# Four graph layers on one core: an order of issue from a planner, replaced by an order written as one mark per operation

## The chip, the cores and the metric

The kernel runs on one core of a Trainium2 chip. The metric is the device time of one execution in microseconds, given as the median of several runs. An execution that the hardware profiler took gives the profile and the trace. The engines are TensorE (PE, with its weight loads as PEld), VectorE (DVE), ScalarE (ACT), GpSimd (POOL) and SyncE (SP), which only issues DMA transfers here.

## The reference

The input `x` is 128 graphs of 64 nodes with 256 features in float32, and `adj` is a 64x64 matrix of zeros and ones for each graph. Four graph layers follow one another, and each is wrapped as `x = layernorm(x + layer(x))`:

```
layer 0: h = x; five times:
             m = h @ weight[l];  agg = A^T m
             r = sigmoid(i_r + h_r);  z = sigmoid(i_z + h_z)
             n = tanh(i_n + r * h_n);  h = (1 - z) * n + z * h
layer 1: agg = eps * x + adj @ x;  h = silu(rmsnorm(agg @ W1 + b1));  out = h @ W2 + b2
layer 2: t = artanh(|x|) * x / |x|;  s = adj @ t
         out = project(tanh(|s|) * s / |s|)
layer 3: h = x @ W^T + b;  u = adj * exp(e_i + f_j + a_b)
         out = (u / sum(u)) @ h
```

In layer 0 `i` and `h` stand for the two products with the recurrent cell's weights, `w_ih` and `w_hh`. Everything is float32.

## The kernel before

Two graphs of 64 nodes make a block of 128 rows, four blocks make a group of 512 rows, and 16 groups cover the input. Each group goes through all four layers on its own. Three sets of buffers (`NF = 3`) let up to three groups be under way together, so that one group's matmuls can lie beside another's vector work. [...]

The Python code does not issue instructions as it goes. Every step (`pe`, `turn`, `dve`, `act`, `pool`, `copied`, `scaled`, L319 to L350) adds an operation, an `Op`, to the list of its stream. Stream 0 prepares constants and weights, and the 16 groups follow as one stream each (L1167 to L1170). An `Op` knows the engines that can do it, an estimated duration, and through `either` (L174) which operations must come before it. Most have one engine. A copy out of PSUM (`copied`, L335 on ACT or L336 on DVE) and a scaling with a bias (`scaled`, L340 on ACT or L341 on DVE) have two, and so have `tan` (L1082, L1083) and `hw` (L1145, L1147).

`Flow.issue` (L225) then sets the order. A planner, `Plan.advance` (L70), keeps an estimated clock for each engine and chooses, again and again, the operation that can start first, among the first few of each engine (`AHEAD`) in four streams (`WINDOW`). Ties and priorities go by one of three ranks. The string `CHOICES` has one digit for each stretch of 5 us of the planner's clock and says which rank holds in it. The operations are issued in that order, and each instruction is tied behind the one before it on its engine (L238), so that the order on every engine, the queue of SP among them, is the planner's. Within this order an engine waits for what its next instruction needs, and everything behind that instruction waits with it.

These steps matter around the change:

- In layer 0 `gated` (L759) runs five times for each group. `gate` (L798) makes the matmuls of L802 into the banks `p_ga`, `p_gb` and `p_gc`; `prod` (L807) those of L808 into `p_hx`, `p_hy`, `p_ix` and `p_iy`. `taken` (L848) and `plus` (L851) bring them into `U` and `V`; `begun` (L819) and `added` (L823) into `hnb`. `sums` (L783) makes the differences `tA` and `tB` on DVE by the helper at L347.
- Between two of the five rounds DVE transposes `h` into `t` (L764), and four DMA transfers on SP (`moved`, L677) bring it into `hr`. `aggregate` (L680) multiplies that by the edges, into `ps_agg`.
- `load` (L375) issues a group's loads on SP: eight of `xs` (L382), four of `x` (L387) and four of `edge` (L391).
- A layer norm (`layer_norm`, L703) takes its statistics from ACT (L716, L719) or, in the last two groups, from DVE (L723 to L725), a power from POOL (L727), and scales the rows (L340 or L341).
- Layer 1 makes `hid` by the matmuls of L985, squares it (L971), scales it on DVE (L1034) and applies the activation on ACT (L1036). The matmuls into `ps_o1` follow (L1044, recorded at the helper's line L317, the name without its digits being `ps_o`).
- POOL adds a bias to whole rows and sums squares by the helper at L350.
- Layer 2 has a logarithm (L1063) and a tanh (L1101) on ACT, each with its own table of functions to be loaded where the table in place has not got it. `tan` (L1082) feeds `ps_sup`.
- Layer 3 takes transposed rows `x3T`, over DMA transfers or in the last two groups by TensorE (`ps_T`, L659), and goes through `ps_a`, `hw` (L1142, L1145) and `ps_att` to the stored rows (L1165).

Of the kernel before, what the change touches and what calls it, by code (L numbers as in the profile page):

```python
# [23 lines left out]
BANKS = 8  # L24


class Buf:


    def __init__(self, make, slot=None, bank=False):  # L30
        self.make, self.slot, self.bank = make, slot, bank
        self.ap, self.uses, self.left, self.after = None, [], 0, ()
# [8 lines left out]


class Op:
    __slots__ = ("eng", "us", "run", "ways", "stream", "n", "kb", "sets", "need", "then", "bufs", "opens", "id", "way", "port")

    def __init__(self, ways, stream, n, kb, sets, port=()):
        self.port = port
        self.ways = {eng: (us, run) for eng, us, run in ways}
        self.eng, self.us, self.run = ways[0]
        self.stream, self.n, self.kb, self.sets = stream, n, kb, sets  # L50
        self.need, self.then, self.bufs, self.opens, self.id, self.way = 0, [], (), None, 0, 0.0


class Plan:


    def __init__(self, flow):
        self.flow = flow
        ops = [o for s in flow.streams for o in s]
        self.need = [o.need for o in ops]  # L60
        self.at = [0.0] * len(ops)
        self.uses = {}
        self.clock = dict.fromkeys(flow.AHEAD, 2.5)
        self.queues = [{e: deque(o for o in s if e in o.ways) for e in self.clock} for s in flow.streams]
        self.banks = [0.0] * BANKS
        self.left, self.first, self.bus = len(ops), 0, 0.0
        self.lands = [0.0] * flow.TRANSFERS
        self.order, self.table, self.port = [], None, 0.0

    def advance(self, until, rank):  # L70


        flow, need, at, clock, banks = self.flow, self.need, self.at, self.clock, self.banks
        while self.left and clock["PE"] < until:
            best = None
            for s in range(self.first, min(self.first + flow.WINDOW, len(self.queues))):
                for e, q in self.queues[s].items():
                    opened = False
                    for _, o in zip(range(flow.AHEAD[e]), q):
                        t = max(clock[e], at[o.id], self.port) if e in o.port else max(clock[e], at[o.id])  # L80
                        if o.opens is not None:
                            if opened or not banks or need[o.id]:
                                opened = True
                                continue
                            t = max(t, banks[0])
                        elif need[o.id]:
                            continue
                        elif o.kb and e != "POOL":
                            t = max(t, self.lands[0])
                        elif o.sets and self.table not in o.sets:  # L90
                            t += flow.TABLE
                        key = (t + flow.SOONER if len(o.ways) > 1 and e == "DVE" else t, *rank(s, o))
                        if best is None or key < best[0]:
                            best = key, o, e, t
            if best is None:
                return False
            _, o, eng, t = best
            if o.sets and self.table not in o.sets:
                self.table = o.sets[0]
            for e in o.ways:  # L100
                self.queues[o.stream][e].remove(o)
            self.order.append((eng, o))
            end = t + o.ways[eng][0]
            clock[eng] = end
            if eng in o.port:
                self.port = end
            if o.opens is not None:
                banks.pop(0)
            for b in o.bufs:
                n = self.uses.get(b, b.left) - 1  # L110
                self.uses[b] = n
                if not n:
                    banks.append(end + flow.hop(eng, "PE"))
                    banks.sort()
            if o.kb:
                self.bus = max(self.bus, end + flow.DMA[0]) + o.kb / flow.DMA[1]
                end = self.bus + flow.DMA[2]
                if o.eng != "POOL":
                    self.lands = [*self.lands[1:], end]
            for u in o.then:  # L120
                need[u.id] -= 1
                at[u.id] = max(at[u.id], end + flow.hop(eng, u.eng))
            self.left -= 1
            while self.first < len(self.queues) and not any(self.queues[self.first].values()):
                self.first += 1
        return True


class Flow:

    AHEAD = {"PE": 32, "DVE": 10, "ACT": 10, "POOL": 4, "SP": 2}


    HOPS = {"from PE": 0.22, "to PE": 0.36, "else": 0.06, "own": 0.0}

    REACH = {"from PE": 0.22, "to PE": 0.15, "else": 0.06, "own": 0.0}

    SOONER = 0.4


    DMA = (2.0, 330.0, 1.0)
    TRANSFERS = 8

    TABLE = 1.28
    WINDOW, STRETCH, LAGS = 4, 5.0, (60.0,)
    CHOICES = ("0110000002200022000010000001110100000000000101100022010011000220121010001100020002021101200021110012"
               "2211210220202220001022000200012200202011010110010000000101100002211011022212100001101010000001011210"
               "0001000010110112002210001201201100100000011000021111000100100010102011000201200012220100000001221100"
               "0010010012010011000000010100000010011021010000010200100021000011011210000100101202022101121200000011"
               "11100101011110111111010001011111100111111111100100010000")  # L160

    BEHIND = mybir.DependencyInfo(mybir.DependencyClass.NoSync, mybir.DependencyReason.DATA)

# [7 lines left out]
    def op(self, eng, us, run, w=(), r=(), kb=0, sets=None, port=False):  # L171
        self.either([(eng, us, run)], w, r, kb, sets, (eng,) if port else ())

    def either(self, ways, w, r, kb=0, sets=None, port=()):  # L174

        o = Op(ways, len(self.streams) - 1, len(self.ops), kb, sets, port)
        before = set()
        for accesses, writes in ((r, False), (w, True)):
# [26 lines left out]
            u.then.append(o)  # L205
        self.ops.append(o)

    def hop(self, e, to, hops=None):
        hops = hops or self.HOPS
        if e == to:  # L210
            return 0.0 if e == "PE" else hops["own"]
        return hops["from PE" if e == "PE" else "to PE" if to == "PE" else "else"]

    def ways(self):

        for i, o in enumerate(o for s in self.streams for o in s):
            o.id = i
        path = {}
        for ops in self.streams:
            longest = 0.0  # L220
            for o in reversed(ops):
                path[o] = o.us + max((path[u] + self.hop(o.eng, u.eng, self.REACH) for u in o.then if u.stream == o.stream), default=0.0)
                o.way = longest = max(longest, path[o])

    def issue(self):  # L225
        self.ways()
        ranks = (lambda s, o: (s, o.n), lambda s, o: (s if o.kb else -s, o.n), *(lambda s, o, lag=lag: (lag * s - o.way, s, o.n) for lag in self.LAGS))
        plan, until = Plan(self), 0.0
        for c in self.CHOICES:
            until += self.STRETCH  # L230
            assert plan.advance(until, ranks[int(c)])
        assert not plan.left
        last = {}
        for eng, o in plan.order:
            made = o.ways[eng][1]()
            for i in made if isinstance(made, list) else [made]:
                if eng in last:
                    self.tc.add_manual_dep(i.ins, last[eng].ins.name, self.BEHIND, reason="the plan's order")  # L238
                last[eng] = i
# [963 lines left out]
```

## Time and profile before

| what | value |
|---|---|
| median of three runs | 2290.74 us (2290.71 to 2294.59) |
| the profiled execution | 2295.18 us, of which the span from first to last instruction is 2293.4 us |
| mean granted TensorE clock | 0.992 |
| busy: PE, DVE, ACT, POOL | 2248.4, 1770.4, 1306.2, 338.3 us |
| matmul instructions | 11242 |
| DMA | 84.20 MB, mean 37 GB/s |

A row of the profile gives a source line, the engine, the operation, what it writes and reads, how often, and how long. After it stands in brackets how long the engine was idle just before, and which instruction's end released it. A row of the order of time begins with the start and the length in microseconds. Matmuls overlap one another, and their ends are modelled: the busy time of PE covers gaps that are shorter than one matmul's length. The starts of consecutive matmuls show those gaps. A line can be that of a helper (L317, L347, L350, L802, L808), so that the names of the tiles tell the rows apart.

### The profile page before, as it was taken

Reading aid. Unit: us, or ns where it says so; the run is one execution under the profiler, and the core shown is the slowest. Engines: PE = TensorE matmul, PEld = TensorE weight load, DVE = VectorE, ACT = ScalarE, POOL = GpSimd, SP = SyncE. Lnnn points to the kernel's source line nnn. Section 1 sums busy time; section 2 is a strip of 40 time slices with the busy share of each in tenths; the row PEclk is TensorE's granted clock in tenths of the full one; section 3 lists DMA queues with packets and bytes.
Section 4 is the critical chain, followed back from the end, with each engine's and each line's share of the span. In section 5 each row is a group of like instructions: output and inputs, shape, how many; then the busy total and the mean of one; then the engine's idle time right before and its main releaser. Section 6 shows DMA issues by size and latency. Waiting matters only on the chain.

```text
span 2293.4 us, 32317 instructions
## 1 busy us (share of the span) xinstructions
PE 2248.4 (98%) x11242; PEld 1978.7 (86%) x11242; DVE 1770.4 (77%) x4167; ACT 1306.2 (57%) x2797; POOL 338.3 (15%) x272
## 2 busy tenths in 40 slices
PE   9999999999999999999999999999999999999985
PEld 6888888888888888888888888888888888888874
DVE  6777788788778777778777878777787877877875
ACT  3444556675565655565655656555565665654665
POOL 3100202310110211112110111211102120110111
PEclk9999999999999999999999999999999999999997
DMA  5221112122112122121211212112131211212110
GB/s 146 33 28 29 28 19 58 19 49 38 40 28 57 21 28 49 19 53 28 31 43 28 49 29 49 28 21 47 28 58 19 36 41 29 49 19 28 22 26 19
DMA packets 428770, 84.20 MB, mean 37 GB/s; under 512 B 399124, under 2 KB 427824, under 8 KB 428608
## 3 DMA queue, kind: packets, MB, share of 16 engines
q1 hardware_dynamic: 426880, 80.26, 19.9%
q8 instruction: 89, 1.46, 0.3%
q10 hardware_dynamic: 1328, 1.31, 0.2%
q0 software_dynamic: 400, 0.57, 0.1%
q14 instruction: 73, 0.60, 0.1%
HBM read 32.55 MB, written 8.39 MB: 18 GB/s over the span
## 4 chain that ended last, share of the span: by engine, by line
PE 93%; DVE 4%; DMA 1%; ACT 1%; issue 0%; SPq 0%; POOL 0%; POOLq 0%; ACTq 0%; DVEq 0%
PE p_ga L802 24%; PE p_gc L802 12%; PE ps_o L317 9%; PE ps_agg L317 7%; PE p_ix L808 6%; PE p_gb L802 6%; PE p_hx L808 6%; PE p_ah L985 4%; PE p_iy L808 4%; PE p_hy L808 4%; PE ps_a L317 2%; PE p_ch L985 2%; PE ps_sup L317 1%; PE ps_wmih L317 1%; PE p_bh L985 1%; PE ps_att L317 1%
## 5 line engine op out<-in xcount | busy, mean ns | idle before, releaser
L727 POOL TENSOR_TENSOR rstd<-ve,pow 128x4 f32<-128x4 f32 (+1 forms) x64 | 76.6, 1197 | 1241.7 <-DVE ve L719 1192.1
L317 PE MATMUL ps_o<-w2s,hid 128*128 128x256 f32 x1024 | 232.4, 382 | 7.0 <-ACT hid L1036 7.0
L317 PEld LDWEIGHTS ps_o<-w2s,hid 128*128 128x128 f32 x1024 | 195.3, 191 | 34.4 <-ACT hid L1036 7.8
L340 ACT ACTIVATE hnb<-p_hx,half_b 128x256 f32<-128x256 f32 x214 | 100.6, 470 | 136.8 <-PE p_hx L808 103.2
L802 PE MATMUL p_gc<-tB,w_a 128*128 128x256 f32 x640 | 172.9, 379 | 1.0 <-DVE tB L347 1.0
L802 PE MATMUL p_ga<-tA,w_h 128*128 128x256 f32 x640 | 172.2, 380 | 0.0
L802 PE MATMUL p_gc<-tA,w_h 128*128 128x256 f32 x640 | 170.2, 379 | 0.0
L802 PE MATMUL p_ga<-tB,w_a 128*128 128x256 f32 x640 | 169.4, 380 | 0.8 <-DVE tB L347 0.8
L802 PE MATMUL p_ga<-hT,w_h 128*128 128x256 f32 x640 | 169.0, 379 | 0.7 <-DVE U L852 0.7
L802 PE MATMUL p_ga<-agg,w_a 128*128 128x256 f32 x640 | 167.5, 379 | 0.0
L317 PEld LDWEIGHTS ps_agg<-edge,hr 128*128 128x128 f32 x1024 | 140.5, 192 | 10.8 <-issue 1.3
L317 PE MATMUL ps_agg<-edge,hr 128*128 128x128 f32 x1024 | 142.9, 276 | 0.3
L855 ACT ACTIVATE U<-U,half_b 128x512 f32<-128x512 f32 (+1 forms) x160 | 94.3, 628 | 83.3 <-DVE U L852 83.2
L802 PEld LDWEIGHTS p_ga<-tB,w_a 128*128 128x128 f32 x640 | 120.7, 190 | 17.7 <-DVE tB L347 1.6
L802 PEld LDWEIGHTS p_gc<-tB,w_a 128*128 128x128 f32 x640 | 120.5, 190 | 17.3 <-DVE tB L347 1.4
L802 PEld LDWEIGHTS p_gc<-tA,w_h 128*128 128x128 f32 x640 | 120.2, 190 | 15.6
L802 PEld LDWEIGHTS p_ga<-agg,w_a 128*128 128x128 f32 x640 | 120.0, 190 | 15.6 <-ACT agg L335 0.2
L802 PEld LDWEIGHTS p_ga<-hT,w_h 128*128 128x128 f32 x640 | 119.0, 190 | 16.0 <-DVE U L852 1.1
L802 PEld LDWEIGHTS p_ga<-tA,w_h 128*128 128x128 f32 x640 | 117.2, 190 | 13.6
L855 ACT ACTIVATE V<-V,half_b 128x256 f32<-128x256 f32 (+1 forms) x160 | 87.8, 586 | 64.5 <-DVE V L852 64.0
L335 ACT COPY agg<-ps_agg 128x512 f32<-128x512 f32 x134 | 77.5, 579 | 62.7 <-PE ps_agg L317 61.5
L868 DVE TENSOR_TENSOR V<-p_ix,V 128x256 f32<-128x256 f32 x192 | 80.5, 420 | 31.1 <-PE p_ix L808 27.8
(259 smaller groups left out, 5480.4 us busy)
## 6 DMA issues: line engine op xcount, KB each, us to landing
hr<-t SPq DMA_DIRECT2D x256, 128.0 KB, 3.8
x<-in_x_dram SPq DMA_DIRECT2D x64, 128.0 KB, 2.6
xr<-in_x_dram SPq DMA_DIRECT2D x16, 512.0 KB, 4.0
out_dram<-x_n SPq DMA_DIRECT2D x16, 512.0 KB, 2.9
xs<-in_x_dram SPq DMA_DIRECT2D x120, 64.0 KB, 2.4
x3T<-t SPq DMA_DIRECT2D x56, 128.0 KB, 3.8
edge<-in_adj_dram SPq DMA_DIRECT2D x64, 32.0 KB, 2.3
wm<-in_L_gnn_weight_dram SPq DMA_DIRECT2D x5, 256.0 KB, 5.1
```

The source lines that it names most:

```text
L317: return nc.tensor.matmul(o, lhsT, rhs, start=(k == 0), stop=(k == nk - 1))
L335: flow.either([("ACT", 0.22 + 0.00077 * n, lambda: nc.scalar.copy(o(), i())), ("DVE", 0.145 + 0.00105 * n, lambda: nc.vector.tensor_copy(o ...
L340: flow.either([("ACT", 0.3 + 0.0008 * n, lambda: nc.scalar.activation(o(), i(), AF.Identity, bias=bias(), scale=scale())), ("DVE", 0.145 + ...
L727: pool(1.25, lambda: nc.gpsimd.tensor_tensor(rstd[:, :m, :], ve[:, :m, :], pow2[:, :m, :NB], OP.pow), [rstd], [ve])
L802: pe(HR, lambda i=i, w=w, c=c: nc.tensor.matmul(ps[:, c * HR:(c + 1) * HR], w[:, m, c * P:(c + 1) * P], v[i][0](), start=first and i == 1 ...
L808: pe(HR, lambda: nc.tensor.matmul(ps[:, j * HR:(j + 1) * HR], w[:, m, :], v[0](), start=first, stop=True, skip_group_check=True), [ps], [( ...
L855: act(HR if len(w) == 1 else R, lambda: nc.scalar.activation(o(), src(), AF.Tanh, bias=half_b[:, i * KD + c:i * KD + c + 1], scale=0.5), w ...
L868: dve(HR + 44, lambda: nc.vector.tensor_add(uu[:, c, half(n)], region(ps, j), uu[:, c, half(n)]), [(uu, (n, c))], [ps, (uu, (n, c))])
L985: pe(HR, lambda c=c: nc.tensor.matmul(ps[:, c * HR:(c + 1) * HR], w1f[:, w, (2 * q + c) * P:(2 * q + c + 1) * P], v[0](), start=first and ...
```

## The change

The planner goes: the class `Plan`, the estimates for hops between engines, DMA transfers and table loads, the ranks, and the string `CHOICES`. In their place stands `ORDER`, a string of marks, one for each operation, in the order of issue. A mark is one of 80 signs, or `~` with two of them for a larger number. It gives an engine, a stream counted from the first one that is not done, and a place among that stream's operations that still wait for that engine. `placed` reads the marks and hands out the operations in turn. The operations themselves, what they need, and the tie behind the one before on the same engine stay as they are. The string has 12850 marks.

```diff
-class Plan:
...
-    def advance(self, until, rank):
...
 class Flow:
...
-    AHEAD = {"PE": 32, "DVE": 10, "ACT": 10, "POOL": 4, "SP": 2}
...
-    WINDOW, STRETCH, LAGS = 4, 5.0, (60.0,)
-    CHOICES = ("0110000002200022000010000001110100000000000101100022010011000220121010001100020002021101200021110012"
...
+    ENGINES, AHEAD = ("PE", "DVE", "ACT", "POOL", "SP"), 6
+    SIGNS = "ABCDEFGHIJKLMNOPQRSTUVWXYZabcdefghijklmnopqrstuvwxyz0123456789!#$%&()*+,-./:;<=>"
+    ORDER = ("EACEDEAACCh#AAhAiDAAAAAAAAE~Bt$Ci~Bt~BOAAE888~Bti~Btli88888iE~BL~EtE~BL~BL~Et~BL~Bt~D8~CU~BLE~CU~DA~"
...
+    def placed(self):
+
+        at, n = self.SIGNS.index, len(self.SIGNS)
+        waiting = [{e: [o for o in s if e in o.ways] for e in self.ENGINES} for s in self.streams]
+        first, marks = 0, iter(self.ORDER)
+        for c in marks:
+            i = at(next(marks)) * n + at(next(marks)) if c == "~" else at(c)
+            i, e = divmod(i, len(self.ENGINES))
+            i, s = divmod(i, self.AHEAD)
+            o, eng = waiting[first + s][self.ENGINES[e]][i], self.ENGINES[e]
+            assert not o.need
+            for u in o.then:
+                u.need -= 1
+            for e in o.ways:
+                waiting[o.stream][e].remove(o)
+            while first < len(waiting) and not any(waiting[first].values()):
+                first += 1
+            yield eng, o
+        assert first == len(waiting)
 
     def issue(self):
-        self.ways()
...
-        plan, until = Plan(self), 0.0
-        for c in self.CHOICES:
-            until += self.STRETCH
-            assert plan.advance(until, ranks[int(c)])
-        assert not plan.left
         last = {}
-        for eng, o in plan.order:
+        for eng, o in self.placed():
             made = o.ways[eng][1]()
```

## The prediction

> **What bounds the kernel now.** I read the page first (engines, slices), then the busy time by stage, then who TensorE waits for, and last the order of time where it waits.
>
> ```profile
> PE 2248.4 (98%) x11242; PEld 1978.7 (86%) x11242; DVE 1770.4 (77%) x4167; ACT 1306.2 (57%) x2797; POOL 338.3 (15%) x272
> PE   9999999999999999999999999999999999999985
> PEclk9999999999999999999999999999999999999997
> ```
>
> TensorE is the bound: 98% busy, and below nine tenths only in the last two of 40 slices. A new order of the same matmuls can win only what lies between them. The busy time by stage (columns: stretch, length, busy time of PE, PEld, DVE, ACT, POOL, granted clock, DMA share, GB/s) says where that is.
>
> ```profile
> 0.00:100.00 100.00, 95.85 (x463) 77.57 (x464) 63.80 (x153) 37.98 (x84) 26.59 (x48) 1.00 0.39 97
> 100.00:2150.00 2050.00, 2043.39 (x10307) 1811.80 (x10306) 1607.08 (x3722) 1185.64 (x2543) 291.50 (x209) 1.00 0.20 35
> 2150.00:2250.00 100.00, 87.68 (x404) 73.81 (x402) 73.55 (x187) 59.87 (x120) 13.02 (x10) 0.95 0.11 22
> 2250.00:2293.00 43.00, 21.44 (x72) 15.52 (x72) 26.00 (x107) 22.69 (x53) 7.18 (x6) 0.68 0.07 25
> ```
>
> Idle: 4.2 us in the first 100, 6.6 in the next 2050, 12.3 in the next 100, 21.6 in the last 43, where the clock also falls. Busy time hides small gaps because matmuls overlap, so I also took the starts of consecutive matmuls: a 128x256 one follows the last after 216 ns, and what exceeds such steady distances is lost. That gives a loss of 4.3 us up to 100; 14.6 from 100 to 2150, of which nine places of over 0.3 us make 7.6 and the rest is crumbs; 12.8 plus 4.4 at half clock from 2150 to 2243; 16.3 plus 5.9 at half clock from there to the last matmul start at 2283.1; and 10.3 after it. Steady matmuls need 2223 us and the first starts at 2.5; that adds up to the span but for rounding.
>
> ```profile
> PE ps_sup L317 <- ACT tan L1082: 8.9, 1, 8.9
> PE ps_o L317 <- ACT hid L1036: 7.0, 3, 4.3
> PE ps_T L659 <- ACT x_n L340: 4.9, 2, 3.5
> ```
>
> The three longest waits all lie after 2190. The 4.3 is an order on DVE, here at its place:
>
> ```profile
> 2192.78 0.74 DVE L944 SCALAR_TENSOR_TENSOR ea<-ident,eps_c,adjT 128x512 f32<-128x512 f32 x1
> ...
> 2194.64 0.39 DVE L723 BATCH_NORM_STATS2 st<-y 128x6 f32<-128x256 f32 x1
> ...
> 2196.41 2.06 DVE L1034 SCALAR_TENSOR_TENSOR hid<-hid,cols,ps_rms 128x512 f32<-128x512 f32 x3
> ```
>
> ```profile
> 2193.01 0.63 PE L669 MATMUL ps_hr<-ident,hT 128*128 128x128 f32 x4
> 2197.97 0.79 PE L317 MATMUL ps_o<-w2s,hid 128*128 128x256 f32 x1 [4.33 <-ACT hid L1036]
> ```
>
> DVE does one group's layer-norm statistics before another group's three `hid`, and TensorE's next matmul needs those `hid`.
>
> **The change part by part.** Decoding the marks by the rule in `placed` gives 5794 PE, 3725 DVE, 2457 ACT, 266 POOL and 608 SP operations. The trace of before has 266 POOL and 608 SP operations too, its 11242 matmul instructions are 5794 operations (two each, a transpose one), and its ACT instructions make 2465 operations. So nothing is added or removed, and net eight operations that either engine can do go from ACT to DVE. A copy costs 0.58 us on ACT (L335) and 0.68 on DVE (L336): 5.4 us more on DVE, hidden under its 23% idle. If that cover failed, 5.4 would be the whole price. I take 0.
>
> How far is the order moved? A POOL mark tells how many PE operations are placed before it, and the trace of before tells how many had started when the same-numbered POOL instruction ran. From the 43rd POOL operation on, the two mostly differ by two or less. The last eight, the powers of the two final groups' norms, stand 70, 48, 44, 40, 40, 21, 3 and 0 PE operations before the end, against some 70, 49, 44, 42, 40, 20, 10 and 0. So the interleave of the groups stays; single steps are shuffled inside it.
>
> *Start* (4.3 lost): weights must land first; I take 0.5 back, ends 0 and 2.
>
> *Middle.* What can return is the 7.6 us of nine places; the crumbs (7.0) are no order. Five of the nine, 4.4 us, follow a stretched DVE instruction:
>
> ```profile
> 1176.41 2.84 DVE L347 TENSOR_TENSOR tB<-agg 128x512 f32<-128x512 f32 x1
> 1179.29 0.42 DVE L347 TENSOR_TENSOR tB<-agg,tB 128x256 f32<-128x256 f32 x1
> ```
>
> ```profile
> 1176.36 2.35 POOL L350 TENSOR_TENSOR xb<-x_n,b_r 128x1024 f32<-128x1024 f32 x1 [4.11 <-ACT x_n L340]
> ```
>
> `tB` takes 2.84 us instead of some 0.68 because POOL began 0.05 us before it, and TensorE lost 1.2. In the whole trace 32 DVE instructions are over 0.3 us above their median, all beside a POOL one, 29.4 us in sum, 0.92 each. [...] by the rows TensorE paid 0.46 to 1.17 in each of the five, mean 0.88, since other groups' matmuls cover the rest. I use 0.88. Half of the 7.6 back is 3.8; ends +7.6 and minus some ten new collisions, -8.8.
>
> *Approach, 2150 to 2243* (17.1 lost). Were the three `hid` (2.06 us) put before the statistics, TensorE would start about 3.5 us earlier, and the other group's chain be 2 us later; L1036 and L985 give several such swaps. The clock counts with it. [...] The trace has it falling at 2162.7 with no gap longer than 1.2 us before it, only several in a row, so the measurement decides: small gaps cost clock too. [...] by the trace it is 17.1. I take half, 8.5; ends 0 and 15.
>
> *Tail, from 2243* (22.2 lost, 10.3 after). It is one group's chain with too little of the other's matmuls beside it.
>
> ```profile
> 2263.75 0.59 ACT L335 COPY x3T<-ps_T 128x512 f32<-128x512 f32 x1 [0.31 <-PE ps_T L659]
> 2264.35 1.28 ACT L1101 ACT_TABLE_LOAD   x1
> 2265.64 0.21 ACT L1101 ACTIVATE th<-n 128x4 f32<-128x4 f32 x1
> ```
>
> The last group's tanh has its input at 2262.3 and stands behind two copies of the other group: before them it would come 1.4 us earlier. Layer-norm rows shared out to DVE (L341, 0.41 us) instead of four on ACT (L340, 2.07 together) give another 1 to 2. I take 3, ends -2 and 7. The 10.3 (residual, norm, store) is a chain in itself: 0.
>
> *DMA queue.* The order on SP can be read from its marks alone, as each group's list is in the code: the four `edge` loads of at least five groups now stand ahead of a block of `hr` transfers that they followed. Behind them wait those `hr`, and behind these `ps_agg`. A block of `edge` issues holds SP 2.6 us, so 13 us at worst, nothing if the SP queue was idle. TensorE's waits name no `hr` now and 1.6 us of `x3T`; two other groups' matmuls lie beside each transfer. I take 0. For new waits anywhere I subtract 2.
>
> **Sum.** 0.5 + 3.8 + 8.5 + 3 - 2 = 13.8 us. The profiled execution took 2295.2 (its span 2293.4), 4.4 over the median 2290.7; from it I get 2281.4, and from the median 2276.9. Forecast 2277.
>
> **Rivals.**
> *Only the middle moves* (2289, chance 0.12). The last groups' phases keep their places, and if the swaps there were no better the end keeps its 39 us: 3.8 - 2, within 0.2%. Against it: the longest waits are so plainly local that single moves reach them.
> *The end closes up* (2261, 0.15): 15 of the approach, 7 of the tail, 7 of the middle, 1 of the start, 30 in all. For it: a fix early in the chain moves all behind it, and the clock stays up. Against it: the unchanged interleave, with too few matmuls left to fill the last 40 us.
> [...] where the shuffled DVE steps fall under POOL's additions (L350, 2.35 us for 128x1024, L350 on `sqt` as well), TensorE pays 0.88 each. If only the middle's gain of 3.8 is had, ten more than now make it slower by over 0.2%; fifteen give 2300. Against it: five reach TensorE today among 256 POOL instructions, which keep their places.
>
> **How the numbers follow.** The forecast's case has 0.65, by itself 2266 to 2286. Faster by over 0.2% (below 2286.2): 0.65 + 0.15 = 0.80; within, 0.12; slower, 0.08. About 0.2% is what measuring this kernel can tell from no change. For 8 in 10 the range leaves out about half of the closed end (0.07), the collisions (0.08) and the upper part of the second case (0.05): 2262 to 2289.
>
> **What would show it.** The wait of `ps_o` for `hid` (7.0) halved and the stretch 2150 to 2243 some 8 us shorter, clock above 0.95 there; the tanh load ahead of the copies; the long waits of the middle at 4 us or less; 32 stretched DVE instructions, give or take ten. It is wrong if the approach keeps 12 us of waits, if TensorE waits for `hr`, or if stretched DVE instructions double.

## The result and the profile after

The changed kernel takes 2282.21 us (median of five runs, 2281.37 to 2283.47), the one before 2290.74 beside it (five runs, 2289.69 to 2294.59). By these medians it is 8.5 us faster. The ratio, of the means, is 0.9961 with a 95% interval of [0.9946, 0.9975], which makes 8.9 us. The profiled execution took 2281.37 us, its span 2279.6. Most line numbers of steps are 66 higher than before.

The page's engines and slices, after:

```profile
PE 2244.8 (98%) x11242; PEld 1974.4 (87%) x11242; DVE 1773.6 (78%) x4175; ACT 1307.2 (57%) x2789; POOL 337.6 (15%) x272
PE   9999999999999999999999999999999999999996
PEclk9999999999999999999999999999999999999997
```

The count of matmuls is the same, eight instructions have gone from ACT to DVE as the marks said, and only the last slice is now below nine tenths. Busy time by stage, after, with the same columns as before:

```profile
0.00:100.00 100.00, 97.34 (x466) 78.96 (x467) 63.92 (x155) 38.14 (x84) 25.90 (x48) 1.00 0.39 97
100.00:2150.00 2050.00, 2045.95 (x10319) 1812.00 (x10318) 1614.10 (x3739) 1188.89 (x2539) 291.28 (x209) 1.00 0.20 35
2150.00:2250.00 100.00, 84.78 (x396) 70.83 (x394) 76.50 (x212) 64.95 (x135) 15.81 (x12) 0.94 0.11 22
2250.00:2280.00 30.00, 16.74 (x64) 12.63 (x64) 19.05 (x71) 15.18 (x34) 4.58 (x4) 0.73 0.10 35
```

A reader could take the third row for a failure: PE is less busy there (84.8 against 87.7) and the clock no higher (0.94 against 0.95). But the row is cut at fixed times, and everything now comes earlier, so that some of the poorly filled tail has moved into it. To compare the same work I used the start of the n-th matmul in both traces. Against before, the 5000th starts 2.1 us earlier, the 10500th (at 2097) 4.0, the 10960th (at 2201) 13.1, the 11120th 10.5 and the last 13.6. So most of what the two traces differ by comes between 2097 and 2201, some is given back behind it, and the tail returns that. Who TensorE waits for, after:

```profile
PE ps_sup L383 <- ACT tan L1148: 8.3, 1, 8.3
PE ps_o L383 <- ACT hid L1102: 4.5, 3, 1.6
...
PE ps_T L725 <- ACT x_n L406: 1.4, 1, 1.4
PE ps_T L725 <- DVE x_n L407: 1.3, 1, 1.3
...
PE ps_rms L1096 <- POOL fac L1093: 0.8, 1, 0.8
```

The 4.3 us wait for `hid` is gone; three of 1.4 to 1.6 are left. The wait for the rows of `x_n` fell from 4.9 to 2.7, now with one row on DVE. A wait for `fac` is new. The order of time on DVE and on TensorE at the place that the prediction showed, now some 8 us earlier:

```profile
2178.52 1.41 DVE L1100 SCALAR_TENSOR_TENSOR hid<-hid,cols,ps_rms 128x512 f32<-128x512 f32 x2
...
2182.50 0.74 DVE L1100 SCALAR_TENSOR_TENSOR hid<-hid,cols,ps_rms 128x512 f32<-128x512 f32 x1
...
2185.48 0.73 DVE L1100 SCALAR_TENSOR_TENSOR hid<-hid,cols,ps_rms 128x512 f32<-128x512 f32 x1
```

```profile
2184.82 1.13 PE L383 MATMUL ps_o<-w2s,hid 128*128 128x256 f32 x4 [1.44 <-ACT hid L1102]
...
2186.23 2.78 PE L383 MATMUL ps_o<-w2s,hid 128*128 128x256 f32 x12
2190.43 1.56 PE L383 MATMUL ps_o<-w2s,hid 128*128 128x256 f32 x6 [1.41 <-ACT hid L1102]
```

Before, one `hid` was scaled and then six steps on `hT`, the rows `y`, `ea` and the statistics followed ahead of the next three. Now two are scaled ahead of the `hT` steps, one among them, one among the statistics. So 12 matmuls stand where TensorE had waited 4.33 us, and a wait of 1.41 us is left behind them. In the tail, on ACT:

```profile
2251.12 1.28 ACT L1167 ACT_TABLE_LOAD   x1
2252.42 0.20 ACT L1167 ACTIVATE th<-n 128x4 f32<-128x4 f32 x1
2252.53 1.06 ACT L401 COPY x3T<-ps_T 128x512 f32<-128x512 f32 x2
```

The tanh and its table load now stand ahead of the two copies.

### The profile page after: what moved, and what is told of

The parts are those of the page before. It is cut to its first block, busy times and chain, and to the rows that moved or that the text cites. A ratio compares the mean times of both kernels' runs of the same rounds, so it can differ in the third digit from the quotient of the medians.

```text
span 2279.6 us, 32289 instructions
## 1 busy us (share of the span) xinstructions
PE 2244.8 (98%) x11242; PEld 1974.4 (87%) x11242; DVE 1773.6 (78%) x4175; ACT 1307.2 (57%) x2789; POOL 337.6 (15%) x272
## 4 chain that ended last, share of the span: by engine, by line
PE 94%; DVE 3%; ACT 1%; DMA 1%; SPq 1%; issue 0%; POOL 0%; POOLq 0%; ACTq 0%; DVEq 0%
PE p_ga L868 23%; PE p_gc L868 11%; PE ps_o L383 10%; PE ps_agg L383 7%; PE p_gb L868 6%; PE p_ix L874 6%; PE p_hx L874 6%; PE p_ah L1051 4%; PE p_iy L874 4%; PE p_hy L874 4%; PE ps_a L383 3%; PE p_ch L1051 2%; PE ps_sup L383 1%; PE ps_wmih L383 1%; PE p_bh L1051 1%; PE ps_att L383 1%
## 5 line engine op out<-in xcount | busy, mean ns | idle before, releaser
L868 PE MATMUL p_gc<-tA,w_h 128*128 128x256 f32 x640 | 175.4, 379 | 0.0
L868 PE MATMUL p_ga<-hT,w_h 128*128 128x256 f32 x640 | 174.3, 380 | 0.2
```

Of the source, the lines that this page charges most:

```text
L868: pe(HR, lambda i=i, w=w, c=c: nc.tensor.matmul(ps[:, c * HR:(c + 1) * HR], w[:, m, c * P:(c + 1) * P], v[i][0](), start=first and i == 1 ...
```

## The experiments

Both orders can be written as marks. There are many places in the two strings at which both have placed the same set of operations, and there one can be continued by the other. I cut behind marks 11967, 12308, 12545 and 12589. In the trace of before, TensorE comes to these cuts at about 2118, 2180, 2226 and 2236 us. "Old" and "new" below are the two strings of 12850 marks. My theory: the gain is in the last groups' phases, where two chains share DVE and ACT, and little of it before the first cut. The first rival: the collisions in the middle, where a DVE instruction is stretched beside a POOL one, give it. The second: it comes from the engines that were exchanged, or from the code that hands out the operations, not from the order. Ratios are to the kernel before on the same chip, with 95% intervals, and gains in microseconds are worked out from them.

**The old order, written as marks.**

```diff
-ORDER = new marks 1 to 12850
+ORDER = old marks 1 to 12850
```

> The order of before written out as marks, so that the instructions and their order are those of before. Every theory expects a ratio of 1.000 within 0.002. What it is for is a second trace of that order: the profiled execution of before took 2295.2 us, 4.4 over the median. If the 4.4 us sits in the approach and the tail (matmul 10700 of 11242 starts within 0.5 us of the 2137 us of before), the gain of the end is overstated by the first pair of traces; if it sits in the middle (matmul 10700 starts some 4 us earlier), the gain of the middle is.

Measured: 2292.23 us, ratio 1.0002 [0.9994, 1.0010]. Writing the order as marks changes nothing that can be measured; the order is the change.

**The new order only up to mark 11967, and only behind it.**

```diff
-ORDER = old marks 1 to 12850
+e_front: ORDER = new marks 1 to 11967, old marks 11968 to 12850
+e_end:   ORDER = old marks 1 to 11967, new marks 11968 to 12850
```

> The new order for the first 11967 of 12850 operations (to about 2115 us), the order of before from there on. My theory (most of the gain comes from the approach, where DVE's order held up ps_o): 4 us faster than before, 2286.7, the 3.8 forecast for the middle and the 0.5 for the start, with the end as long as it was. Rival (the order earns its gain evenly along the run, and the end of the first trace was an accident of that execution): all or nearly all of the 8.5 us, 2282 to 2283.

> The order of before for the first 11967 operations, the new one from there on. My theory: what the whole change gained less what the front gains, 4.5 us by the medians, 2286; by the two traces alone it would be 9. Rival (even gain, the end an accident): within 1 us of before.

Measured: e_front 2290.79 us, 0.9996 [0.9988, 1.0005], that is 0.9 us [-1.1, 2.7]. e_end 2286.59 us, 0.9971 [0.9961, 0.9982], that is 6.6 us [4.1, 8.9]. The front brings less than the 4 us that I expected. The last 7% of the marks bring most of the gain, some 70 to 90% by these two runs, whose intervals are wide.

**Three `hid` moved ahead, and nothing else.** This is the prediction's step by itself: in the old order the three scalings on DVE (its G marks here) go ahead of `ea` and of the other group's statistics.

```diff
-HLFL~F3L,KKK,KLLLLLLLLLLGNGHGHFLH~FZGFMG
+HLFL~F3LGGG,KKK,KLLLLLLLLLLNHHFLH~FZGFMG
```

> The order of before with three operations moved: the three hid scalings on DVE that stood behind the other group's statistics now stand ahead of ea and those statistics. My theory, as in the prediction: TensorE's ps_o starts some 3.5 us earlier, the half-clock stretch at 2197 shrinks or goes, and the run is 3 to 4 us faster, 2287. Rival: the group whose statistics are put back by 2.06 us is the last one, its chain sets the end, and the gain is given back: the ps_o wait goes, but the end stays within 1 us.

Measured: 2293.69 us, 1.0005 [0.9997, 1.0014]. No gain. The order of time of DVE and then of TensorE in this kernel says why:

```profile
2192.29 2.05 DVE L1093 SCALAR_TENSOR_TENSOR hid<-hid,cols,ps_rms 128x512 f32<-128x512 f32 x3
```

```profile
2193.83 2.43 PE L376 MATMUL ps_o<-w2s,hid 128*128 128x256 f32 x10 [0.69 <-ACT hid L1095]
2199.95 2.07 PE L376 MATMUL ps_agg<-ea,x_n 128*128 128x128 f32 x8 [3.69 <-ACT x_n L399]
```

The ten `ps_o` matmuls start at 2193.83 instead of 2197.97 and wait 0.69 us. But then TensorE stands 3.69 us before `ps_agg`, whose `x_n` come from the other group's statistics. ACT in the kernel before and, in the second fence, in this one:

```profile
2197.19 2.04 ACT L1036 ACTIVATE hid<-hid,cols 128x512 f32<-128x512 f32 x3 [5.42 <-DVE hid L1034]
2199.13 2.06 ACT L340 ACTIVATE x_n<-y,off,rstd 128x256 f32<-128x256 f32 x4
```

```profile
2199.30 2.08 ACT L399 ACTIVATE x_n<-y,off,rstd 128x256 f32<-128x256 f32 x4 [4.21 <-DVE off L790]
```

Before, `x_n` stood behind the three `hid` on ACT; now it waits for its own statistics, which DVE makes later, and it starts no earlier. The wait was handed from one chain to the other. From the second cut to the third TensorE takes 45.7 us here, and 45.2 to 46.3 us in six traces of the old order.

**The end in parts.** The new order only from mark 11968 to 12308, only from 12309 to 12545, and only behind 12545:

```diff
-ORDER = old marks 1 to 12850
+e_appr: ORDER = old 1 to 11967, new 11968 to 12308, old 12309 to 12850
+e_late: ORDER = old 1 to 12308, new 12309 to 12545, old 12546 to 12850
+e_tail: ORDER = old 1 to 12545, new 12546 to 12850
```

> The order of before, but for operations 11967 to 12308 (about 2115 to 2178 us) the new one. My theory: it takes away about 1.6 us of waits before 2165 and with them, in some executions, a half-clock window of 3.4 us: 1 to 2 us faster, 2290. Rival (each small gap costs clock in every execution): 3.3 us faster, 2288.4.

> The order of before, but for operations 12308 to 12545 (about 2178 to 2225 us) the new one: there it removes the 4.5 us wait of ps_o. My theory after the first experiments: the wait was the lack of other work beside two chains, and half of what this stretch saves is lost again behind it (the new trace gives 2.4 us back at the next ps_o), so 1 to 3 us faster, 2289 to 2291 beside a before of 2291.7. Rival, the prediction's own step: the whole 5 us stay, 2286.5.

> The order of before up to operation 12545 (about 2225 us), the new one for the last 305: the tanh of the last group ahead of the other group's copies, the logarithm's table loaded between the row scalings, rows shared out to DVE. My theory: the tail is one chain and keeps all that is taken out of it, 3 us by the prediction and 4 to 5 by the traces: 2287 to 2288.5. Rival (the tail only shifts idle time: the stores wait for DVE instead): within 1 us of before.

Measured: e_appr 2290.38 us, 0.9986 [0.9980, 0.9993], 3.2 us; e_late 2290.12, 0.9988 [0.9981, 0.9994], 2.7 us; e_tail 2292.35, 0.9997 [0.9989, 1.0005], 0.7 us. Together 6.6 us, as much as e_end, though the interval of each is about 1.5 us to either side. Each part of the approach gains by itself; the tail does not bring the 3 to 5 us that I expected. The 3.2 us of e_appr is the rival's number, but not for the rival's reason. From the first cut to the second TensorE takes 58.0 us in its trace. With the old order there, five traces take 60.0 to 60.6 us at full clock, and the three that fall to half clock at about 2162 us (in before the clock is 0.50 from 2162.72 to 2166.13) take 61.9 to 62.1. So the gain is some 2 us, and 3.8 where the clock had fallen. e_appr alone still has the wait of 4.3 us for `hid`, e_late alone none for it over 2.0.

**Only the engines exchanged.** The new order gives 18 operations to another engine, 13 from ACT to DVE and 5 the other way. Here the old order has these 18 and nothing else of the new one. One of the 18 marks, from DVE to ACT:

```diff
-FMGFGF(~B:L~B:H
+FMHFGF(~B:L~B:H
```

> The order of before with nothing moved, but the eighteen operations that the new order gives to another engine given to it (thirteen from ACT to DVE, five back). My theory: nothing by itself, within 1 us of before, since the gain comes from the order of steps. Rival: sharing out the rows of the last norms between ACT and DVE is what shortens the tail, and this alone gives 2 us or more.

Measured: 2293.98 us, 1.0007 [0.9999, 1.0015]. No gain: in this trace the waits of `ps_T` fall from 4.9 to 3.4 us and those of `ps_att` grow by 0.5. Whether the shared rows help at their new places is not shown by itself.

**The tail without its first 44 marks.** In e_tail the trace shows two more steps of `ps_o` ahead of `ps_ss`; these are marks 12546 to 12589. Here the tail goes without them, and in a second kernel the changed one has the old order in them.

```diff
-ORDER = old marks 1 to 12850
+e_tail2: ORDER = old 1 to 12589, new 12590 to 12850
+e_mix:   ORDER = new 1 to 12545, old 12546 to 12589, new 12590 to 12850
```

> The order of before, but the new one for the last 261 operations, from 12589 on; e_tail had it from 12545 and gained nothing. My theory: the tail's own moves (tanh ahead of the copies, the logarithm between the scalings, rows shared out) are worth 3 to 4 us, and the 44 operations ahead of them took that away: 3 us faster than before. Rival: the tail's moves are worth nothing without an earlier end of the chain, within 1 us of before.

> The new order, but for operations 12545 to 12589 (about 2214 to 2222 us in the changed kernel) that of before, which keeps two more ps_o steps of one group behind the other group's ps_ss, as filler for its wait. My theory: this stretch is where the change loses (a wait of 0.96 for the power plus 1.76 for hid, against one of 2.16, and a half-clock window in each of its traces so far), so 0.6 to 2.4 us faster than the changed kernel. Rival: the window comes from waits that either order has, and the two are within 0.5 us.

Measured: e_tail2 2289.53 us, 0.9990 [0.9984, 0.9997], 2.3 us. e_mix 2282.32, 0.9960 [0.9947, 0.9972]. TensorE in e_tail and, in the second fence, in e_tail2:

```profile
2227.84 0.65 PE L1090 MATMUL ps_rms<-ident,fac 128*128 128x128 f32 x4 [0.80 <-POOL fac L1087]
2230.08 6.26 PE L377 MATMUL ps_o<-w2s,hid 128*128 128x256 f32 x14 [1.59 <-ACT hid L1096]
```

```profile
2225.22 0.65 PE L1090 MATMUL ps_rms<-ident,fac 128*128 128x128 f32 x4
2227.86 8.47 PE L377 MATMUL ps_o<-w2s,hid 128*128 128x256 f32 x38 [2.00 <-ACT hid L1096]
```

With the 44 marks, work is used up early that would have stood beside `fac`, so `ps_rms` waits for it. In the first kernel 14 matmuls take 6.26 us, and the clock from 2224 to 2236 is 0.72; in the second 38 take 8.47, and it is 1.00. But undoing the 44 marks in the changed kernel brings nothing: there a wait of `ps_ss` for `sqt` (0.89 us) comes in, the wait for `hid` is 1.99, and the clock from 2215 to 2236 is 0.92 in both. The 0.6 to 2.4 us that I expected did not come; the rival was right.

**The changed kernel again.**

```diff
 ORDER = new marks 1 to 12850
```

> The changed kernel again, for a second trace and a larger sample. If the parts add up (front 0.9, the three stretches of the end 2.1, 2.4 and 0.2 us), it is 5.6 us faster than before, ratio 0.9976. If the stretches help one another (my theory: the waits of the tail are only worth taking out once the chains ahead of it are short), it stays at 8 us or more, 0.9965 or less. By the forecast's own sum it would be 13.8, 0.994.

Measured: 2282.63 us, 0.9960 [0.9948, 0.9972], 9.2 us. By their ratios the two series give 8.9 and 9.2. The parts, e_front, e_appr, e_late and e_tail, make 7.5 together. The interval of the whole is 6.4 to 11.9 us, so these times do not tell whether the parts add up or help one another.

**GpSimd's additions in halves.** The changed kernel, with each 128x1024 addition on POOL done as two of 128x512; the sums are the same.

```diff
-pool(..., lambda: nc.gpsimd.tensor_tensor(o(), x0(), x1(), op), w, r)
+pool(..., lambda: [nc.gpsimd.tensor_tensor(o()[:, v, :], x0()[:, v, :], x1()[:, v, :], op)
+                   for v in (slice(0, 2), slice(2, 4))], w, r)
```

> The changed kernel with each of POOL's additions of 128x1024 made in two halves of 128x512 (the same sums). [...] the six or seven stretches of 2 us or more in DVE go down to about 1.1, while POOL works a little longer. The time of the run: within 1 us of the changed kernel, since in its middle only the wait at 455 us (0.96) still follows a collision. Rival [...]: 2 us faster.

Measured: 2283.05 us, 0.9960 [0.9946, 0.9974], within 0.5 us of the changed kernel. The same DVE operation on `hT` beside POOL's `xb`, in the changed kernel and then in this one:

```profile
608.49 2.61 POOL L416 TENSOR_TENSOR xb<-x_n,b_r 128x1024 f32<-128x1024 f32 x1 [4.70 <-ACT x_n L406]
608.80 2.85 DVE L413 TENSOR_TENSOR hT<-hT,U 128x512 f32<-128x512 f32 x1
```

```profile
608.90 1.77 DVE L413 TENSOR_TENSOR hT<-hT,U 128x512 f32<-128x512 f32 x1
610.70 1.65 DVE L995 SCALAR_TENSOR_TENSOR hT<-V,hT 128x512 f32<-128x512 f32 x1
```

2.16 us above its usual 0.69 become 1.08, and the second half hits the next instruction. Over the whole trace the longest excess falls from 2.16 to 1.12 us, while the sum (34.4 us in 32 instructions, now 31.1 in 40) falls little and the time stays. So this run shows how long one stretch is, and not what the collisions cost; the 2 us that would have come if they were what is left of the middle's loss did not. The two waits of TensorE that follow a collision in the changed kernel, 1.0 us at 455 and 1.3 us at 2141 by the starts of the matmuls, are there in this one too. At the second of them, DVE in the changed kernel and then in this one:

```profile
2137.27 2.29 DVE L1173 TENSOR_TENSOR th<-th,rn 128x4 f32<-128x4 f32 x1
```

```profile
2138.36 1.20 DVE L1177 TENSOR_TENSOR th<-th,rn 128x4 f32<-128x4 f32 x1
2139.60 1.19 DVE L1178 TENSOR_TENSOR n<-th,n 128x4 f32<-128x4 f32 x1
```

The two halves of POOL's `xb` hold up two operations of one chain, for about as long as the whole had held up one.

## Why the prediction was nearly right

The forecast was 2277 and the time is 2282.2: 13.8 us off were expected and 8.5 came (8.9 by the ratio). The likeliest case happened and none of the rivals, and the mechanism was the one forecast: the interleave of the groups stays, single steps are moved, and most of the gain comes from the waits of the last two groups. The sum was too large by some 4 us. That it equals the difference of the two *profiled* executions almost to the tenth (2295.18 - 2281.37 = 13.8) is luck: before's profiled execution was 4.4 us above its median, and part of what I took for loss was that one execution's. In the trace of e_same, the same order, the last matmul starts 4.6 us earlier than in before's, of which 1.4 lie ahead of the 10700th and 3.2 behind it.

The experiments' traces allow the sum to be made again over more than one execution. The table has TensorE's time from its first operation behind one cut to its first behind the next, as a mean of the traces that have the old or the new order there. e_hidfirst, e_eng and e_halves are left out, and in the two middle rows also traces in which the order changes between these rows.

| marks | old order, us (traces) | new order, us (traces) | gain | forecast |
|---|---|---|---|---|
| 1 to 11967 | 2117.5 (7) | 2114.9 (4) | 2.6 | 4.3, start and middle |
| 11968 to 12308 | 60.7 (6) | 58.1 (5) | 2.7 | 8.5, approach, with the next row |
| 12309 to 12545 | 45.9 (5) | 41.3 (3) | 4.6 | |
| 12546 to 12589 | 9.4 (5) | 12.1 (3) | -2.8 | -2, new waits |
| 12590 to the last matmul | 47.1 (5) | 44.8 (6) | 2.3 | 3, tail |
| behind the last matmul | 10.2 (5) | 10.1 (6) | 0.2 | 0 |

That makes 9.6 us, against the 8.9 and 9.2 of the two series by their ratios.

- *Start and middle* (0.5 + 3.8). This term was over-sized the most. Timed by itself, e_front gives 0.9 [-1.1, 2.7]; the traces give 2.6. The list of nine places was one execution's. Counted in the same way up to 2110 us, the places of over 0.3 us make 7.0 in before's trace, the most of eight traces with the old order (mean 6.1), and 3.6 on average in four with the new one. A wait of 1.7 us for `x3T` that before's trace has is missing in that of e_same. Four of the five collision waits are gone. The collisions themselves are not: 32 stretched DVE instructions as before, 34.4 us instead of 29.4, but only two waits of TensorE of over 0.5 us follow them, of 1.0 and 1.3 us.
- *Approach* (8.5). The traces give 7.3. Timed, e_appr and e_late give 3.2 + 2.7 = 5.9, by their intervals some 4 to 8; in that, e_late has already lost 1.7 us again behind its own marks (11.1 us in the fourth row, where the old order takes 9.4). The step "three `hid` put before the statistics, TensorE about 3.5 us earlier" is right for its first wait and wrong for the time: e_hidfirst starts `ps_o` some 4 us earlier and gains nothing, because `ps_agg` of the other group then waits. I had written that the other chain would be 2 us later. Its statistics were (the power `rstd` starts at 2198.06 instead of 2196.57), but its `x_n` had been waiting for ACT and came when they had come before, and that already was too late. The new order fills the gap by more, earlier `hid`. As for the clock, before's trace lost 1.8 us in a half-clock stretch at 2162 which e_same, the same order, does not show. My sum counted it as there in every execution.
- *Tail* (3). The traces give 2.3 and e_tail2, timed, 2.3 [0.7, 3.7], with the tanh ahead of the copies as forecast. About right.
- *New waits* (-2). They came, 2.8 us between marks 12546 and 12589: `ps_rms` waits for `fac`, and the clock falls to half at about 2220 us in after (0.50 from 2220.11 to 2223.52), e_end and e_new, which it does not do there with the old order. These marks are not the cause by themselves. Where they are the old ones behind a new approach, in e_late and e_mix, the stretch still takes 11.1 us, and e_mix is no faster than the changed kernel. So it is the earlier approach that runs into these chains; part of its gain is given back. The difference of e_tail and e_tail2 (1.6 us, with intervals that overlap) shows only that the new marks cost something behind an old approach.
- *Engine changes* (0) and *SP's `edge` loads* (0): right. e_eng shows no gain from the first. TensorE waits 0.2 us in all for `hr`.

Of the signs named for the stretch from 2150 to 2243, the clock's came, the length's nearly, and that of the wait for `hid` did not. Its matmuls take 85.6 us instead of 93.0, 7.4 less where some 8 were forecast, though in e_same, with the old order, they take 90.1. The clock there is above 0.95, third from the end in these rows of before and after:

```profile
2150.00:2243.00 93.00, 83.22 (x385) 70.21 (x384) 70.43 (x174) 56.70 (x110) 11.70 (x8) 0.94 0.12 23
```

```profile
2150.00:2243.00 93.00, 81.00 (x388) 68.31 (x386) 72.03 (x193) 59.56 (x119) 14.53 (x10) 0.97 0.12 23
```

That says little of the order, for e_same has 0.98 there. The wait of `ps_o` for `hid` was not halved (7.0 to 4.5), though its longest fell from 4.3 to 1.6. In the middle, the places of over 0.3 us make 4.4 us, where 4 or less were forecast.

## What to carry to other kernels

A long wait on the bound engine is not a prize of its own length: look who is next late, and price a swap only after both chains that share the helper engine have been followed. Make the sum against several executions of the kernel before, not one, when the gain sought is near its spread. And when a kernel is 98% busy on one engine, look at its end first: 7% of the operations held most of this gain.

## What the runs showed of the hardware

**The clock falls in some executions and not in others, for the same order.** Here are rows of busy time in a stretch, with the granted clock third from the end: before, then e_same, each from 2160 to 2170.

```profile
2160.00:2170.00 10.00, 8.79 (x40) 7.09 (x39) 6.07 (x16) 6.59 (x17) 0.00 (x0) 0.83 0.08 10
```

```profile
2160.00:2170.00 10.00, 9.36 (x51) 8.36 (x52) 6.94 (x18) 8.09 (x21) 1.02 (x1) 1.00 0.00 0
```

And the changed kernel, then e_new, which has the same order, each with the same wait of 0.8 us for `tB`:

```profile
455.00:460.00 5.00, 4.94 (x25) 3.99 (x25) 4.93 (x13) 3.71 (x12) 1.02 (x1) 1.00 0.51 80
```

```profile
455.00:460.00 5.00, 4.62 (x16) 3.85 (x17) 3.94 (x11) 2.82 (x8) 1.02 (x1) 0.66 0.60 94
```

Half-clock stretches last 3.41 us or a multiple (but for the last of an execution, which its end cuts off), and within one execution they start whole multiples of 3.413 us apart (after: 2220.11, 2240.59, 2271.3, which are 6 and 9 of them; the clock in each is 0.50). The question is then whether the clock goes with how a few small gaps lie in such intervals.

In the traces it does. The starts of the half-clock stretches give the grid, with intervals of 3.413 us, for a whole execution. For each interval at full clock, without the first 12 us and the last two intervals, I took the share that steady matmuls fill, at the 216 ns by which their starts mostly differ in the traces for a 128x256 one, and in proportion to the columns. In the 14 traces, 52 intervals are filled to less than 0.37, and half clock follows each of them. It follows six of the nine intervals from 0.37 to 0.38, and one of the 9128 above that. At about 2158 us the interval is filled to 0.37 or 0.38 in the three traces whose clock falls there (before, e_hidfirst, e_tail), and to between 0.42 and 0.67 in the five others with the old order there. At 452 us it is 0.375 in e_new and 0.41 or more in the 13 others. So in these traces the same gaps cost clock or not by where the grid lies on them. The share is worked out from the starts and not read from a counter, and no run set the phase.

Such a half-clock stretch cost 1.4 us at 455, where e_new falls from 0.6 to 2.0 us behind the changed kernel's trace, and some 1.7 us at 2162. Over 117 executions of the kernel before, the time goes with the mean granted clock:

| mean granted clock | executions | mean time, us |
|---|---|---|
| 0.991 | 9 | 2295.4 |
| 0.992 | 64 | 2292.7 |
| 0.993 | 18 | 2292.1 |
| 0.994 | 26 | 2290.7 |

The rounded clock accounts for about half of the variance between executions (0.52), and from the first row to the last the time falls by 4.7 us, half of what the change is worth.

**A stretched DVE instruction ends just after the POOL instruction beside it.** Of the 32 in the changed kernel's trace, each starts 0.05 to 1.29 us after the POOL instruction did and ends 0.02 to 0.56 us after it has ended. Halving the POOL instruction halved the longest stretch (2.16 to 1.12 us), and even a 128x4 operation, `th` beside `xb`, takes 2.29 us instead of 0.16 in the changed kernel. Some 4 us later `p_ix` waits 1.1 us for `U`, a wait that the kernel before does not have.
